# Local attention in smaller blocks: 32 queries by 64 keys in place of 64 by 96, one score tile a chunk, and a pipeline of four stations in place of five

## The chip, the cores and the metric

The kernel runs on one core of one Trainium2 chip. A core has a matrix engine (TensorE, PE in the profile, with PEld for its weight loads), three engines for elementwise work (VectorE or DVE, ScalarE or ACT, GpSimd or POOL), and SyncE (SP), which here only issues transfers. The metric is the device time of one launch in microseconds, and less is better. The three timed runs of the kernel before took 3015.64, 3015.70 and 3017.27 us; their median is 3015.7 us.

## The reference

Two blocks are computed for 4 sequences of 512 tokens with 128 features, all in float32. The first holds a gated scan, a mixture of experts and a causal attention; it is not touched by the change except in how two of its PSUM tiles are named. The second, where most of the time goes, is six layers of local attention with 16 heads of 64 features, each followed by a small feed-forward network. This is its attention:

```python
def local_attention(q, k, v):              # window w = 32
    bq, bk, bv = blocks of 32 tokens
    bk2, bv2 = (look(bk), look(bv))        # each block with the one ahead of it: 64 keys
    mask = (it < jb) | (it > jb + w) | (jb == -1)
    sim = einsum('bhwie,bhwje->bhwij', bq, bk2) * 8.0
    attn = softmax(where(mask, -max, sim), -1)
    return einsum('bhwij,bhwje->bhwie', attn, bv2)

def attn_layer(x, Wqkv, qs, ksc, Wo):
    q, k, v = split(x @ Wqkv, 3)           # 16 heads x 64 each
    q, k = l2norm(q) * qs, l2norm(k) * ksc
    q = q*cos*scale + rotate_half(q)*sin*scale
    k = k*cos/scale + rotate_half(k)*sin/scale
    return local_attention(q, k, v) as rows of 1024, @ Wo
```

A query i sees the keys from i - 32 to i. The layer's input is `x` with half its features shifted by one token, and its output is added to `x`. The feed-forward network is a layer norm, a gated GELU of width 341 and a product back to 128 features, added to the same state.

## The kernel before

The state of each sequence lies transposed in SBUF (`sA[b]`, 128 features by 513 columns). A layer is worked in chunks of 128 tokens, so there are 6 layers x 4 sequences x 4 chunks = 96 chunks (`Chunk`). A loop of 96 + 4 rounds (line 786) makes one new chunk a round and moves five chunks a station further; `xe` is the newest and `xa` the oldest. The order in which the loop calls the methods is the order of the instructions on every engine: lines 858 to 863 tie each instruction to the one before it on its engine. So nothing overtakes, and an instruction that waits holds up all that stands behind it on its engine.

What a chunk goes through:

- `rotate(j)`, j = 2, 3 for the keys and 0, 1 for the queries, 8 heads each. One 128x512 product on PE into PSUM (line 539, tile `q`, tag `mm`), two multiplications on DVE (`lt`, lines 547 and 551), their sum on POOL (`ro`, line 556), the squares on ACT (`sq`, line 558, after the DVE readers), and their sums by head on DVE (`ss`, line 559). `norms` raises the sums to the power -1/2 on POOL (line 569), and `scale_keys` multiplies the keys on POOL (line 576).
- `values(j)`: two more 128x512 products (line 586), copied by ACT into `vr` (line 590). `spread` issues three transfers on SP's queue (lines 595 to 597), which lay the keys' values of each block of 64 queries, 96 rows, at partition 0 (`vk`, two sets).
- `window` and `turn(j)`: four 128x128 transposes a call on PE (line 134, tile `tp_r`, tag `tr`) and one copy to `qT` or `kT`.
- `scores(g)`, for 8 heads at a time: a mask is put into two PSUM banks by two bf16 products with an identity (line 621, tag `S`), and 16 products of 64 features x 64 queries x 96 keys are added (line 630). `lm` is the row maximum of 8 heads (line 637) and `lnb` its scaled negative. `exponentials` calls ACT once a head, 128x96 (line 650).
- `flip(g, k)`: four transposes, one head each (line 662, tag `tr`), and a copy of 96x512 to `lpT` (line 516).
- `weigh(g)`: 16 products of 96 keys x 64 queries x 65 columns (line 674, tag `S`); the 65th column gives the sum. DVE divides (`lr` line 680, `on` line 682).
- `lift(j)`: four transposes and a copy by ACT to `oT`; `project`: 8 products with `Wo` (line 698) and two additions to `sA` (line 704).

`feedforward` is a generator of eight parts. It starts once the last chunk of a sequence has been projected, and `advance()` runs one part at fixed places, eight places in four rounds; so its work comes once in four rounds.

[...] Tags `mm` and `tr` have two tiles of one bank each, tag `S` two tiles of two banks. A tile is handed out again only when all readers of its former content are done. A product in float32 shows as two records on PE, and a transpose as one.

Of the kernel before, what the change touches and what calls it, by code (L numbers as in the profile page):

```python
# [35 lines left out]
QB = 64  # L36
# [25 lines left out]
M_BAND = 4 * KB  # L62
# [4 lines left out]
def fused(ctx: ExitStack, tc: tile.TileContext, a: dict, out: bass.AP):  # L67
# [7 lines left out]
    def psum(tag, name):  # L75
        return pp.tile([P, 2, 512] if tag == "S" else [P, 512], F32, tag=tag, name=name)
# [68 lines left out]
    with ExitStack() as stage:  # L145
# [153 lines left out]
        def expert_out(b, e, hT, pr, acc):  # L299
            y = psum("S", f"y{b}_{e}")  # L300
# [26 lines left out]
    with ExitStack() as stage:  # L327
# [39 lines left out]
        def softmax(b, h):  # L367
# [6 lines left out]
            for i2 in range(NC // 2):  # L374
                S = psum("S", f"gs{b}_{h}_{i2}")
# [73 lines left out]
    with ExitStack() as stage:  # L449
# [20 lines left out]
        vr = [sp.tile([P, HEADS, DH + 1], F32, name=f"vr{i}") for i in range(2)]  # L470
        vk = [[sp.tile([KB, HEADS, DH + 1], F32, name=f"vk{i}_{k}") for k in range(2)] for i in range(2)]
        for v in vr:
            nc.vector.memset(v[:, :, DH : DH + 1], 1.0)
        for v in vk:
            nc.vector.memset(v[0], 0.0)
# [42 lines left out]
        class Chunk:  # L518


            def __init__(self, n, l, b, c, w, last):
# [4 lines left out]
                self.VK = vk[n % 2]  # L526
                self.ss = sm.tile([P, 2 * HEADS], F32, tag="ss", name=f"ss{self.tag}")
                self.rot = {}
                self.S = {}
                self.nb = {}  # L530
                self.P = {}
                self.pT = {}
                self.on = {}

            def rotate(self, j):

                tag = f"{self.tag}_{j}"
                q = psum("mm", f"q{tag}")
# [3 lines left out]
                )  # L542
                cs = self.w["rot"][:, 2 * (j // 2), self.c, :]
# [13 lines left out]
                sq = wk.tile([P, 512], F32, tag="sq", name=f"sq{tag}")  # L557
                nc.scalar.activation(sq, q, AF.Square)  # L558
                nc.vector.tensor_reduce(  # L559
                    self.ss[:, j * 8 : j * 8 + 8], heads(sq), AX.X, ALU.add  # L560
# [23 lines left out]
            def values(self, j):  # L584
# [5 lines left out]
                nc.scalar.copy(self.V[:, j * 8 : j * 8 + 8, 0:DH], heads(v))  # L590

            def spread(self):

                if self.c:
                    nc.sync.dma_start(self.VK[0][0:WIN], self.last.V[P - WIN :])
                nc.sync.dma_start(self.VK[0][WIN:], self.V[0:QB])
                nc.sync.dma_start(self.VK[1], self.V[QB - WIN :])

            def window(self):

                self.qT = wk.tile([P, HEADS // 2, P], F32, tag="qT", name=f"qT{self.tag}")
# [14 lines left out]
            def scores(self, g):  # L616

                gt = f"{self.tag}_{g}"
                S = psum("S", f"ls{gt}")[:, :, 0 : 4 * KB]
# [4 lines left out]
                S = S.rearrange("p a (s k) -> p a s k", s=4)  # L624
                for s in range(4):
                    for blk in range(2):

                        for par in range(2):
                            lo, to = par * 64, blk * QB
                            nc.tensor.matmul(  # L630
                                S[to : to + QB, par, s, :],
                                lhsT=self.qT[lo : lo + 64, 4 * g + s, to : to + QB],
                                rhs=self.kT[lo : lo + 64, 4 * g + s, to : to + KB],
                                start=False, stop=s == 3,
                            )
                m = sm.tile([P, 4, 2], F32, tag="lm", name=f"lm{gt}")
# [3 lines left out]
                nb = sm.tile([P, 8], F32, tag="lnb", name=f"lnb{gt}")  # L640
                nc.vector.tensor_tensor(  # L641
                    nb, m.rearrange("p s a -> p (s a)"), self.rq[:, 8 * g : 8 * g + 8], ALU.mult
                )
                self.S[g], self.nb[g] = S, nb
                self.P[g] = wk.tile([P, 8, KB], F32, tag="lp", name=f"lp{gt}")

            def exponentials(self, g, of):
# [138 lines left out]
        for i in range(len(todo) + 4):  # L786
# [29 lines left out]
            if xb:  # L816
                xb.lift(0)
# [151 lines left out]
```

## Time and profile before

One execution was profiled. Its own time was 3016.47 us, and the span from its first to its last instruction 3014.7 us.

| | busy us | share of the span |
|---|---|---|
| PE (matmul) | 2558.3 | 85% |
| PEld (weight loads, beside PE) | 1679.1 | 56% |
| DVE | 1950.1 | 65% |
| ACT | 1476.6 | 49% |
| POOL | 1401.7 | 46% |
| one stretch of four rounds of the layers (1502.40 to 1594.60 us) | 92.2 | |

The mean granted TensorE clock was 0.933. The layers begin at 746.8 us with the first `q` product, and fill the rest of the span. There the work repeats every four rounds. Busy shares count a matmul from its start to its modelled end, so records that overlap each other count once; the rate at which products start is read from the times at which groups of them begin.

### The profile page before, as it was taken

The numbers are of one execution on the slowest core, as the hardware profiler recorded it, in microseconds if no ns is written. First come the engines' busy times: TensorE is split into PE (matmuls) and PEld (weight loads), VectorE is DVE, ScalarE is ACT, GpSimd is POOL, SyncE is SP. The second block draws the span as 40 slices with busy tenths as digits, with TensorE's granted clock in tenths as the row PEclk, the third lists the DMA queues.
The fourth block names the chain that finished last, engine by engine and source line by source line (L and its number), as shares of the span: only waits on it lengthen the run. The fifth ranks groups of instructions, "written<-read, shape, count | busy, mean of one in ns | idle before, by whom it ended". The sixth has DMA issues, their size and how long they took to land.

```text
span 3014.7 us, 56751 instructions
## 1 busy us (share of the span) xinstructions
PE 2558.3 (85%) x22640; PEld 1679.1 (56%) x22640; DVE 1950.1 (65%) x4218; ACT 1476.6 (49%) x3417; POOL 1401.7 (46%) x1002
## 2 busy tenths in 40 slices
PE   3899888887779888888888898888888888988886
PEld 1567545554456555555555565555555555655553
DVE  6344466666676666766667666666666676666764
ACT  1111133333556555555555565555555555655553
POOL 2000011111766555665556555565655565555550
PEclk7799989999899999999999999999999999999998
DMA  5000000000112111121112111121111211111110
GB/s 168 1 1 1 1 1 1 1 1 1 42 32 77 32 31 33 42 67 33 31 40 67 33 42 31 31 68 41 32 32 32 75 34 31 41 32 31 37 37 17
DMA packets 44963, 103.92 MB, mean 34 GB/s; under 512 B 5526, under 2 KB 23196, under 8 KB 43804
## 3 DMA queue, kind: packets, MB, share of 16 engines
q1 hardware_dynamic: 41852, 97.27, 12.3%
q8 instruction: 178, 2.92, 0.4%
q10 hardware_dynamic: 2848, 3.03, 0.3%
q14 instruction: 85, 0.70, 0.1%
HBM read 25.75 MB, written 1.05 MB: 9 GB/s over the span
## 4 chain that ended last, share of the span: by engine, by line
PE 33%; DVE 22%; ACT 17%; issue 2%; ACTq 0%; DMA 0%; DVEq 0%; POOL 0%; POOLq 0%
PE q L539 7%; PE ly L698 6%; ACT lp L650 6%; PE lv L586 5%; DVE lt L547 5%; ACT sq L558 5%; PE tp_r L134 4%; DVE lt L551 4%; DVE ss L559 3%; PE ls L630 3%; DVE lm L637 3%; DVE on L682 2%; PE lo L674 2%; PE lpt L662 2%; PE tp_on L134 1%
## 5 line engine op out<-in xcount | busy, mean ns | idle before, releaser
L556 POOL TENSOR_TENSOR ro<-lt,lt 128x512 f32<-128x512 f32 x384 | 487.5, 1270 | 721.8 <-DVE lt L551 369.3
L558 ACT ACTIVATE sq<-q 128x512 f32<-128x512 f32 x384 | 232.1, 604 | 644.8 <-DVE lt L551 603.1
L650 ACT ACTIVATE lp<-ls,lnb,rn 128x96 f32<-128x96 f32 x1536 | 529.0, 450 | 4.1 <-DVE lnb L641 3.8
L559 DVE TENSOR_REDUCE ss<-sq 128x8 f32<-128x512 f32 x384 | 263.3, 686 | 352.4 <-ACT sq L558 352.4
L539 PE MATMUL q<-wqkv,sA 128*128 128x512 f32 x768 | 430.5, 644 | 4.7 <-DVE fh L738 2.9
L134 PEld LDWEIGHTS tp_r<-ident,ro 128*128 128x128 f32 x1536 | 197.6, 151 | 265.4 <-issue 156.0
L547 DVE TENSOR_TENSOR lt<-q,rot 128x512 f32<-128x512 f32 x384 | 265.4, 691 | 106.4 <-PE q L539 105.0
L134 PE MATMUL tp_r<-ident,ro 128*128 128x128 f32 x1536 | 254.8, 293 | 81.9 <-DVE st_f L115 48.1
L662 PEld LDWEIGHTS lpt<-ident,lp 128*96 128x96 f32 x1536 | 180.6, 130 | 242.3 <-issue 139.6
L569 POOL TENSOR_TENSOR rn<-rn,neg_half 128x16 f32<-128x16 f32 x96 | 278.9, 2905 | 64.9 <-DVE rn L566 64.8
L569 POOL TENSOR_TENSOR rk<-rk,neg_half 128x16 f32<-128x16 f32 x96 | 278.8, 2905 | 27.6 <-DVE rk L566 27.6
L662 PE MATMUL lpt<-ident,lp 128*96 128x128 f32 x1536 | 233.4, 282 | 64.0 <-DVE lpT L516 60.8
L551 DVE TENSOR_TENSOR lt<-q,rot 128x512 f32<-128x512 f32 x384 | 261.0, 680 | 0.0
L516 DVE COPY lpT<-lpt 96x512 f32<-96x512 f32 x288 | 192.0, 681 | 105.6 <-PE lpt L662 105.5
L630 PE MATMUL ls<-kT,qT 64*64 64x96 f32 x6144 | 185.7, 262 | 53.7 <-ACT qT L516 53.7
L674 PE MATMUL lo<-vk,lpT 96*64 96x65 f32 x6144 | 223.8, 225 | 1.1 <-ACT lpT L516 1.1
L630 PEld LDWEIGHTS ls<-kT,qT 64*64 64x64 f32 x6144 | 149.8, 142 | 128.3 <-issue 65.5
L698 PE MATMUL ly<-oT,lwo 128*128 128x128 f32 x1536 | 194.4, 280 | 26.9 <-ACT vr L590 26.9
L674 PEld LDWEIGHTS lo<-vk,lpT 96*64 96x64 f32 x6144 | 197.0, 138 | 35.7 <-issue 34.3
L586 PE MATMUL lv<-wqkv,sA 128*128 128x512 f32 x384 | 207.4, 644 | 3.2 <-ACT sq L558 3.2
L590 ACT COPY vr<-lv 128x512 f32<-128x512 f32 x192 | 113.8, 593 | 179.4 <-PE lv L586 179.4
L698 PEld LDWEIGHTS ly<-oT,lwo 128*128 128x128 f32 x1536 | 178.9, 192 | 37.8 <-ACT vr L590 32.5
(178 smaller groups left out, 4195.8 us busy)
## 6 DMA issues: line engine op xcount, KB each, us to landing
vk<-vr SPq DMA_DIRECT2D x96, 390.0 KB, 4.0
vk<-vr SPq DMA_DIRECT2D x96, 260.0 KB, 3.4
vk<-vr SPq DMA_DIRECT2D x72, 130.0 KB, 2.3
wqkv<-in_lwqkv_dram SPq DMA_DIRECT2D x6, 1536.0 KB, 10.0
ew<-in_ew_dram SPq DMA_DIRECT2D x16, 256.0 KB, 6.3
lwo<-in_lwo_dram SPq DMA_DIRECT2D x6, 512.0 KB, 10.9
lw<-in_lw_dram SPq DMA_DIRECT2D x6, 341.0 KB, 10.2
cst<-in_cst_dram ACTq DMA_DIRECT2D x1, 1028.0 KB, 5.3
```

Of the source, the lines that this page charges most:

```text
L134: nc.tensor.transpose(tp[:, c * P : (c + 1) * P], i[:, c, :], ident)
L539: nc.tensor.matmul(q, lhsT=self.xs, rhs=self.w["qkv"][:, j * 512 : (j + 1) * 512], start=True, stop=True,)
L547: nc.vector.tensor_tensor(heads(t1), heads(q), cs[:, None, :].to_broadcast([P, 8, DH]), ALU.mult)
L551: nc.vector.tensor_tensor(swapped(t2), swapped(q)[:, :, ::-1, :], sn[:, None].to_broadcast([P, 8, 2, 32]), ALU.mult,)
L556: nc.gpsimd.tensor_tensor(self.rot[j], t1, t2, ALU.add)
L558: nc.scalar.activation(sq, q, AF.Square)
L569: nc.gpsimd.tensor_tensor(r, r, neg_half.to_broadcast([P, HEADS]), ALU.pow)
L630: nc.tensor.matmul(S[to : to + QB, par, s, :], lhsT=self.qT[lo : lo + 64, 4 * g + s, to : to + QB], rhs=self.kT[lo : lo + 64, 4 * g + s, t ...
L650: nc.scalar.activation(self.P[g][:, i, :], self.S[g][:, i % 2, i // 2, :], AF.Exp, bias=self.nb[g][:, i : i + 1], scale=self.rq[:, 8 * g + ...
L662: nc.tensor.transpose(pt[0:KB, i * P : (i + 1) * P], self.P[g][:, 4 * k + i, :], ident)
L674: nc.tensor.matmul(o[to : to + QB, i // 4, i % 4, :], lhsT=self.pT[g][:, i, to : to + QB], rhs=self.VK[blk][:, 8 * g + i, :], start=True, ...
L698: nc.tensor.matmul(y, lhsT=self.w["o"][:, j, :], rhs=self.oT[:, j, :], start=j == 0, stop=j == INNER // P - 1,)
```

## The change

The blocks become 32 queries by 64 keys (`QB` 32, `NB` 4 blocks a chunk). With 64 keys, two heads of one block fill 128 partitions.

- `mask` opens one tile `S` for all 16 heads with two bf16 products of 512 columns. `scores(g)` adds 32 products of 64 features x 32 queries x 64 keys for 8 heads, and `largest` takes one maximum over 1024 columns and one `lnb` for 16 heads. Each exponential is 128x64.
- `flip(g)` transposes two heads at once, four transposes for 8 heads and two calls a chunk in place of four; its copy is 128x512.
- `weigh(g)` is 32 products of 64 keys x 32 queries x 65 columns. `vk` is one set of four tiles with two heads' halves on 128 partitions, and `spread` issues ten transfers a chunk (eight for the first chunk of a sequence) in place of three.
- In PSUM `S` and `o` have one tile of two banks each. `qT`, `lp` and `lpT` in SBUF have one buffer each.
- `rotate` is split: `query` holds the product and the squares on ACT, which now stand ahead of the two DVE multiplications that read the same PSUM tile.
- The rounds have four stations (`xp` queries, `xt` turns, `xs` scores and values, `xw` weighing and projection), 96 + 3 in all, with a new order. One `lift` copy, and one `turn` copy and one `flip` copy in every fourth round, are on DVE.
- `feedforward` takes its statistics from the SBUF copy `n` in place of the PSUM tile, and its gates' tile from `o`.

```diff
-QB = 64
+QB = 32
+NB = P // QB
-M_BAND = 4 * KB
+M_BAND = 8 * KB
     def psum(tag, name):
-        return pp.tile([P, 2, 512] if tag == "S" else [P, 512], F32, tag=tag, name=name)
+        if tag in ("S", "o"):
+            return pp.tile([P, 2, 512], F32, tag=tag, name=name, bufs=1)
+        return pp.tile([P, 512], F32, tag=tag, name=name)
...
-            y = psum("S", f"y{b}_{e}")
+            y = psum("So"[e % 2], f"y{b}_{e}")
...
-                S = psum("S", f"gs{b}_{h}_{i2}")
+                S = psum("So"[i2], f"gs{b}_{h}_{i2}")
...
-            def rotate(self, j):
+            def query(self, j):
                 tag = f"{self.tag}_{j}"
-                q = psum("mm", f"q{tag}")
+                self.q[j] = q = psum("mm", f"q{tag}")
                 nc.tensor.matmul(
                     q, lhsT=self.xs, rhs=self.w["qkv"][:, j * 512 : (j + 1) * 512],
                     start=True, stop=True,
                 )
+                self.sq[j] = wk.tile([P, 512], F32, tag="sq", name=f"sq{tag}")
+                nc.scalar.activation(self.sq[j], q, AF.Square)
+
+            def rotate(self, j):
+                tag, q = f"{self.tag}_{j}", self.q[j]
...
                 nc.gpsimd.tensor_tensor(self.rot[j], t1, t2, ALU.add)
-                sq = wk.tile([P, 512], F32, tag="sq", name=f"sq{tag}")
-                nc.scalar.activation(sq, q, AF.Square)
                 nc.vector.tensor_reduce(
-                    self.ss[:, j * 8 : j * 8 + 8], heads(sq), AX.X, ALU.add
+                    self.ss[:, j * 8 : j * 8 + 8], heads(self.sq[j]), AX.X, ALU.add
                 )
...
             def spread(self):
-                if self.c:
-                    nc.sync.dma_start(self.VK[0][0:WIN], self.last.V[P - WIN :])
-                nc.sync.dma_start(self.VK[0][WIN:], self.V[0:QB])
-                nc.sync.dma_start(self.VK[1], self.V[QB - WIN :])
+                for par in range(2):
+                    lo = par * KB
+                    if self.c:
+                        nc.sync.dma_start(vk[0][lo : lo + WIN], self.last.V[P - WIN :, par])
+                    nc.sync.dma_start(vk[0][lo + WIN : lo + KB], self.V[0:QB, par])
+                    for r in range(1, NB):
+                        k0 = r * QB - WIN
+                        nc.sync.dma_start(vk[r][lo : lo + KB], self.V[k0 : k0 + KB, par])
...
+            def mask(self):
+                self.S = S = psum("S", f"ls{self.tag}")
                 for par in range(2):
                     nc.tensor.matmul(
                         S[:, par], lhsT=ident_h, rhs=bands[min(self.c, 1)], start=True, stop=False
                     )
+            def scores(self, g):
+                S = self.S.rearrange("p a (s k) -> p a s k", k=KB)
+                for s in range(4 * g, 4 * g + 4):
+                    for r in range(NB):
                         for par in range(2):
-                            lo, to = par * 64, blk * QB
+                            lo, to = par * 64, r * QB
                             nc.tensor.matmul(
                                 S[to : to + QB, par, s, :],
-                                lhsT=self.qT[lo : lo + 64, 4 * g + s, to : to + QB],
-                                rhs=self.kT[lo : lo + 64, 4 * g + s, to : to + KB],
+                                lhsT=self.qT[lo : lo + 64, s, to : to + QB],
+                                rhs=self.kT[lo : lo + 64, s, to : to + KB],
...
+            def flip(self, g, engine):
+                pt = psum("tr", f"lpt{self.tag}_{g}")
                 for i in range(4):
+                    s = 4 * g + i
                     nc.tensor.transpose(
-                        pt[0:KB, i * P : (i + 1) * P], self.P[g][:, 4 * k + i, :], ident
+                        pt[:, i * P : (i + 1) * P],
+                        self.P[:, 2 * s : 2 * s + 2, :].rearrange("p a k -> p (a k)"), ident,
                     )
...
             def weigh(self, g):
+                o = psum("o", f"lo{self.tag}_{g}")[:, :, 0 : 4 * (DH + 1)]
+                for i in range(4):
+                    for r in range(NB):
+                        for par in range(2):
+                            lo, to = par * KB, r * QB
+                            nc.tensor.matmul(
+                                o[to : to + QB, par, i, :],
+                                lhsT=self.pT[lo : lo + KB, 4 * g + i, to : to + QB],
+                                rhs=vk[r][lo : lo + KB, 4 * g + i, :], start=True, stop=True,
+                            )
...
-            stats = statistics(chunks(tp), f"f{tag}")
+            stats = statistics(n, f"f{tag}")
...
-            two = psum("S", f"fg{tag}")
+            two = psum("o", f"fg{tag}")
```

The new round, which replaces lines 786 to 854:

```python
for i in range(len(todo) + 3):
    ...
    xw, xs, xt, xp = (at(i - k) or idle for k in (3, 2, 1, 0))
    k = (i - 3 - 3) % NC
    xs.mask(); xw.weigh(0); xw.divide(0); xs.scores(0)
    xw.weigh(1); xw.divide(1); xs.scores(1); xs.largest(); xt.window()
    xs.values(0); xw.lift(0, nc.scalar); xs.exponentials(range(4)); xp.query(2)
    xw.lift(1, nc.vector); xp.rotate(2); xs.values(1); xs.spread(); xs.exponentials(range(4, 8))
    xt.turn(2, nc.scalar); xp.query(3); xs.exponentials(range(8, 12))
    xp.rotate(3); xp.scale_keys(); xt.turn(3, nc.scalar); xw.project()
    xp.query(0); xs.exponentials(range(12, 16)); xp.rotate(0); xt.turn(0, nc.scalar)
    if k in (0, 1, 2): advance()
    xt.turn(1, nc.vector if k == 1 else nc.scalar)
    if k in (1, 2): advance()
    xp.query(1); xs.flip(0, nc.vector); xp.rotate(1); xp.scale_queries()
    if k in (0, 2, 3): advance()
    xs.flip(1, nc.vector if k == 1 else nc.scalar)
```

## The prediction

> **What bounds the kernel now.** I read the page's busy table and chain first, then the groups, then the timeline of PE over one round, then DVE and ACT in the same window, then the waits.
>
> ```profile
> PE 2558.3 (85%) x22640; PEld 1679.1 (56%) x22640; DVE 1950.1 (65%) x4218; ACT 1476.6 (49%) x3417; POOL 1401.7 (46%) x1002
> ...
> PE 33%; DVE 22%; ACT 17%; issue 2%; ACTq 0%; DMA 0%; DVEq 0%; POOL 0%; POOLq 0%
> ```
>
> PE is the fullest engine, but the chain changes engine often: PE waits for others every round.
>
> ```profile
> 1506.48 1.02 PE L539 MATMUL q<-wqkv,sA 128*128 128x512 f32 x2
> 1507.34 0.60 PE L662 MATMUL lpt<-ident,lp 128*96 128x128 f32 x4
> 1507.78 1.95 PE L698 MATMUL ly<-oT,lwo 128*128 128x128 f32 x16
> 1509.57 0.60 PE L134 MATMUL tp_r<-ident,ro 128*128 128x128 f32 x4
> ...
> 1511.39 1.15 PE L674 MATMUL lo<-vk,lpT 96*64 96x65 f32 x32
> 1512.48 0.66 PE L134 MATMUL tp_on<-ident,on 128*128 128x128 f32 x4
> 1512.97 0.49 PE L621 MATMUL ls<-mask_h,ident_h 128*128 128x384 bf16 x2
> 1513.73 0.89 PE L630 MATMUL ls<-kT,qT 64*64 64x96 f32 x32 [0.27 <-ACT qT L516]
> 1514.56 1.12 PE L539 MATMUL q<-wqkv,sA 128*128 128x512 f32 x2
> ```
>
> From start to start, a 128x512 float32 product takes PE 0.86 us, four transposes 0.44, `ly` 1.79, a weighing group 1.09, the mask pair about 0.49, a score group 0.83. A round without feed-forward sums to 16 us: six products 5.2, 16 turns' transposes 1.75, 16 of `lpt` 1.75, 8 of `tp_on` 0.98, masks 0.98, scores 1.66, weighing 2.18, `ly` 1.79. The maxima at 830.34, 850.52 and 870.71 us give 20.2 us for such a round. With the feed-forward network four rounds take 92.2 us (1503.61 to 1595.77), 23.0 each. The difference of 4 us is waiting and the lowered clock:
>
> ```profile
> 1502.40:1594.60 92.20, 80.95 (x826) 53.66 (x826) 63.30 (x127) 53.86 (x125) 53.94 (x38) 0.94 0.14 35
> ...
> ACT sq L558 <- DVE lt L551: 603.1, 264, 5.4
> DVE ss L559 <- ACT sq L558: 352.4, 384, 2.4
> PE tp_r L134 <- DVE st_f L115: 48.1, 21, 2.7
> DVE lt L547 <- PE q L539: 105.0, 239, 2.1
> ```
>
> The columns of the first line are PE, PEld, DVE, ACT, POOL, clock, DMA share, GB/s. The waits show a serial chain in each `rotate`: product, two DVE passes, square on ACT, sum on DVE.
>
> [...] the 32 score records begin (0.89 - 0.24) / 31 = 21 ns apart although a 96-column stream needs 80 ns (0.83 ns a column, from 0.86 us for two records of 512), which is 80 over 4 tiles. Weighing, with 2 tiles, shows (1.15 - 0.22) / 31 = 30 ns against 54 / 2. [...] `tp_on` behind weighing takes 0.49 against 0.44. [...]
>
> **The change, part by part.** *Small products.* 64 columns are 53 ns, over 8 tiles 6.7 ns a record. A group of 64 records is 0.45 us. Four groups stand together: 1.8 us [...], against 3.84; saved 1.8. The 8-tile form is not in this trace. If only 4 tiles run at once a group is 0.9, and the four are 3.6, a saving of nothing; I take 0.45, as both present groups follow the number of tiles. *Flips*: two calls fewer, 0.88. *Mask*: two 512-column products for four of 384, about 0.6 against 0.98, 0.38. Together PE needs 3.1 us less a chunk, 295 us over 96. That is what the change brings if PE's stalls stay as they are.
>
> *DVE.* One maximum of 1024 columns: 947 ns at 768 and 686 at 512 give 1.02 ns a column, so 1.21 against 1.9. Flips: from three copies to one, plus one of `lift`, 0.6 less. DVE then needs 12.4 us in a plain round. *ACT*: an exponential falls from a place of 0.32 us ((2.68 - 0.45) / 7) by 32 columns of 0.83 ns (368 ns at 128 columns, 688 at 512, line 390) to about 0.30; I use 0.31; 0.3 us a chunk less. *POOL* keeps 13.3 us (four sums 1.27, two powers 2.9, two scalings 1.04, one copy 0.40).
>
> *SP.* Ten transfers a chunk for three. They are issued 0.57 us apart (480 to 545 ns each), and 130 KB land after 2.3 us. The first needs only the last chunk's values; nine wait for the second value copy, behind which nothing but later weights stands on SP. 8 x 0.57 + 2.3 to 4 = 6.9 to 8.6 us after that copy. `vk` has one set, so weighing of the next round waits for it, with mask ahead of it and scores behind.
>
> *Order and buffers.* I walked one plain round by the new order, with PE's result read 0.27 us after its stream (1506.48 + 0.86 to `lt` at 1507.61), 0.61 a DVE place of 512 columns and 0.69 to its result, 0.46 to 0.49 an ACT place and 0.6 to its result. Zero is DVE's end of the round before; weighing 0 is done by then.
>
> DVE divides until 0.92; `o` has one tile, so weighing 1 starts at 0.97; DVE divides again 1.70 to 2.62; maximum to 3.75, `lnb` 3.94. PE goes on with value product, `tp_on`, query 2, `tp_on` to 4.62. ACT: copies to 4.07, four exponentials to 5.30, and only then `sq` 2 to 5.90. The square now stands ahead of DVE's readers, so `lt` starts at 5.93 and ends at 7.22. Query 3 needs that PSUM tile: 7.27 to 8.13; its square, behind four exponentials and a copy, ends at 9.0; DVE to 10.32, sum and `rk` to 10.95. `ly` ends 10.36; query 0 10.37 to 11.23; additions to `sA`; square to 12.10; DVE 12.13 to 13.96. ACT: four exponentials to 13.22, the `qT` copy to 13.80. `flip` 0 needs that PSUM tile: PE 13.85 to 14.29, DVE 14.56 to 15.17, then `rotate` 1 to 17.0 and `rn`. **The plain round is 17.1 us at full clock**, and it is DVE's chain through ACT and PE that closes it, with 4.7 us of gaps on DVE. Values land at about 14 to 15 and are needed at 15.3; POOL's 13.3 fit.
>
> The feed-forward parts stand in the last third of the round: in the first of four rounds statistics (4 x 0.45) and normalise (4 x 0.31) on DVE make 20.0; in the second `xn`, three gate products, the GELUs with a table load of 1.28 and two more DVE copies make 21.8; in the third a table load back (1.2 late on ACT), three more products and three DVE passes make 20.7; in the fourth `fy` and two passes of 0.75 make 18.6. Sum 81.1. About 7.6 us of each walk is PE time; at the granted 0.94 that is 0.4 more a round: **82.7 for four rounds against 92.2**.
>
> 23 such groups save 9.5 each, 218 us; the first rounds without feed-forward save some 2.7 each, about 11. The first block stays: `S` and `o` alternate as two `S` tiles did. The tail after the last projection (2974.4 us to the end, 40 us) is the same generator. One station less is worth nothing sure, as filling rounds are short. 230 us off 3016.5, the profiled execution, is 2786; against the median of 3015.7 it is **2785**.
>
> **The rivals.**
> - *PE stays the bound and its waits go too.* For it: DVE would be at 14.2 of 18.5 us, so a better fit than my walk is possible, and `tp_r` no longer stands behind `st_f`, 48.1 us in all. PE needs 16 - 3.1 + 2.1 (feed-forward, a quarter of 8.6) = 15.0, at 0.94 16.0; with 2.3 of waits 18.3 a round: 4.7 x 95 = 447 less, 2570. Against it: one-buffer tiles and squares behind exponentials.
> - *Values come late.* With a landing of 5 to 6 us more than reckoned (ten transfers sharing engines with each other; before, the longest of the three landed after 4.0), weighing starts at 19 or so in plain rounds: two us more in the plain ones, one in the others, 1.5 x 95 = 140 back: 2925. For it: single `vk`, under one round of slack against over one before.
> - *Slower: small tiles do not run eight at a time.* If a record starts only each 28 ns, two tiles at a time, a group is 1.8 us. PE, from `flip` 0 at 13.85 through mask and three groups to the maximum, then gets it at 22.9 where the walk had 19.6: 3.3 more a round, 24.0 against 23.0, and 3015.7 + 95 = 3110. [...] Against it: 21 ns already seen.
> - *No change* would need the waits to eat exactly what PE gives up.
>
> **How the numbers follow.** Chances: the walk 0.58, with its own range 2690 to 2880 (1 us a round either way); PE-bound and freer 0.16 (2570 to 2690); late values or another one-buffer wait 0.16 (2870 to 3005); slower 0.08; within 0.2%, which is about what a measurement here can tell from no change, 0.02. Two in ten are left out: the lower case under 2620 (0.05), the late case over 2940 (0.05), no change and slower (0.10). Faster 0.90, same 0.02, slower 0.08.
>
> **What would show it.** Right: score and weighing records 7 to 9 ns apart on average, a group some 0.45 to 0.6 us; four rounds of 80 to 86 us; DVE over 68% busy in the layers and PE's share by its records no higher; `lt` waiting for `sq` where `sq` waited for `lt`; DVE waiting for `lpt` and `lo`. Wrong: the first `lo` record waiting for a transfer by more than a us a round (late values), groups of 0.9 us or more (tiles not concurrent), [...] or rounds of 18 us with PE full.

## The result, and the profile after

The changed kernel takes 2993.7 us, the median of four runs (2989.2 to 3001.6), against 3015.7 us before: a ratio of 0.9929, with a 95% interval of 0.9907 to 0.9951. It is faster by 22 us where 230 were forecast. The profiled execution took 2995.5 us, its span 2993.6 us at a mean granted clock of 0.927.

These are the busy row and the shares of the chain on the page of the kernel after.

```profile
PE 2364.7 (79%) x33872; PEld 1536.6 (51%) x33968; DVE 1971.8 (66%) x3977; ACT 1357.4 (45%) x3275; POOL 1398.2 (47%) x1002
...
DVE 25%; PE 21%; ACT 20%; issue 5%; POOL 2%; DMA 1%; SPq 0%; DVEq 0%; POOLq 0%; ACTq 0%
```

DVE is now ahead of PE on the chain, as forecast. PE gave up 194 us of busy time, less than the 295 reckoned. DVE's busy time should have fallen: one maximum of 1024 columns in place of two of 768 takes 65 us less over all chunks, the copies of `lpT`, `qT` and `oT` 27 less, and `lnb` 14 less, together 106 us. It rose by 22.

Four rounds from one maximum to the fourth after it, in the table of stretches (PE, PEld, DVE, ACT and POOL busy, clock, DMA share, GB/s):

```profile
1505.35:1594.28 88.93, 71.54 (x1295) 46.93 (x1299) 64.33 (x117) 48.60 (x117) 53.75 (x37) 0.96 0.19 49
```

This stretch is a good one: 22.2 us a round, where all 95 rounds from the first to the last maximum have a mean of 22.8. The forecast was 82.7 for four, 20.7 a round. So 2.1 us a round, 200 us in all, is what has to be found.

The waits that answer to those shown before:

```profile
PE lo L688 <- DVE on L699: 211.7, 96, 5.7
DVE oT L519 <- PE tp_on L137: 192.5, 96, 5.0
ACT sq L544 <- PE q L539: 145.0, 148, 2.1
DVE lr L697 <- PE lo L688: 131.8, 98, 5.4
DVE lt L552 <- ACT sq L544: 126.4, 160, 1.8
```

`lt` waits for `sq` where `sq` waited for `lt`. PE stands 2.2 us a round ahead of the second weighing group, which needs the first division. And two small groups have grown (busy us, mean ns, idle before):

```profile
L569 DVE TENSOR_SCALAR rn<-ss 128x16 f32<-128x16 f32 x96 | 86.7, 903 | 3.3
L569 DVE TENSOR_SCALAR rk<-ss 128x16 f32<-128x16 f32 x96 | 76.8, 800 | 3.3
```

They are the same 16-column instructions as before, where they took 174 ns in the median (line 566; min/median/max in ns, first and last start in us):

```profile
L566 DVE TENSOR_SCALAR rk<-ss x96: 174/174/177, 754.3 to 2920.7; 128x16 f32<-128x16 f32 x96
L566 DVE TENSOR_SCALAR rn<-ss x96: 174/174/1115, 759.7 to 2935.8; 128x16 f32<-128x16 f32 x96
```

That is about 130 us more of DVE: the 106 us saved above, and the rise of 22.

**One plain round against the walk.** Only the first few of the 95 rounds are plain, but it was a plain one that the prediction walked in full. DVE's timeline of the second round without feed-forward, from its maximum to the next (start, us, idle before):

```profile
803.33 1.23 DVE L652 TENSOR_REDUCE lm<-ls 128x16 f32<-128x1024 f32 x1
804.59 0.18 DVE L656 TENSOR_TENSOR lnb<-lm,rn 128x16 f32<-128x16 f32 x1
806.63 0.69 DVE L519 COPY oT<-tp_on 128x512 f32<-128x512 f32 x1 [1.86 <-PE tp_on L137]
807.75 0.69 DVE L552 TENSOR_TENSOR lt<-q,rot 128x512 f32<-128x512 f32 x1 [0.43 <-ACT sq L544]
...
813.66 0.69 DVE L552 TENSOR_TENSOR lt<-q,rot 128x512 f32<-128x512 f32 x1
...
815.96 0.69 DVE L519 COPY lpT<-lpt 128x512 f32<-128x512 f32 x1 [0.42 <-PE lpt L675]
...
818.48 1.00 DVE L569 TENSOR_SCALAR rn<-ss 128x16 f32<-128x16 f32 x1
819.39 0.19 DVE L697 RECIPROCAL lr<-lo 128x8 f32<-128x8 f32 x1
819.62 0.69 DVE L699 TENSOR_TENSOR on<-lo,lr 128x512 f32<-128x512 f32 x1
821.65 0.21 DVE L697 RECIPROCAL lr<-lo 128x8 f32<-128x8 f32 x1 [1.34 <-PE lo L688]
821.90 0.69 DVE L699 TENSOR_TENSOR on<-lo,lr 128x512 f32<-128x512 f32 x1
822.52 1.23 DVE L652 TENSOR_REDUCE lm<-ls 128x16 f32<-128x1024 f32 x1
```

Counted from the maximum (the walk had it at 2.54 from its own zero, and 17.1 for the round):

| | walk | measured | late by |
|---|---|---|---|
| `oT` copy | 2.35 | 3.30 | 0.95 |
| `lt` of query 0 | 9.59 | 10.33 | 0.74 |
| `flip` 0 copy | 12.02 | 12.63 | 0.61 |
| first division (`lr`) | 14.55 | 16.06 | 1.51 |
| second division | 16.25 | 18.32 | 2.07 |
| next maximum | 17.10 | 19.19 | 2.09 |

The whole middle of the round, four `rotate` calls and a flip, ran as walked, or 0.3 us shorter. The time is lost in three places: between the maximum and `oT` (0.95), at `rn` (0.82 more than the 0.09 that the walk gave it), and between the two divisions (2.26 for 1.70).

**At `rn`.** The timeline of DVE and POOL there:

```profile
818.18 2.48 POOL L561 TENSOR_TENSOR ro<-lt,lt 128x512 f32<-128x512 f32 x2
818.48 1.00 DVE L569 TENSOR_SCALAR rn<-ss 128x16 f32<-128x16 f32 x1
```

The row merges two sums of 1.24 us on POOL; the first ends at 819.4, and `rn` ends at 819.48. Of the 96 `rn`, 95 began while POOL was busy with a sum or a scaling and ended within 40 ns of the end of that instruction; of the 96 `rk`, 94. The two multiplications ahead of them also overlap POOL's work and keep their 0.68 us. So a 16-column instruction that begins beside one of POOL's sums or scalings lasts until that ends; the two that began beside its power (one `rn`, one `rk`) kept 0.17 us. In the kernel before POOL was idle at that moment (94 of 96 `rn`, all 96 `rk`).

**Behind the weighing wait.** The stretch around the waiting group and the value product behind it, and one of the same round without such a wait:

```profile
800.50:805.50 5.00, 4.33 (x135) 3.21 (x136) 2.75 (x5) 0.61 (x2) 3.49 (x3) 0.66 0.07 17
815.00:819.00 4.00, 2.95 (x137) 2.34 (x138) 3.54 (x6) 1.78 (x4) 3.92 (x4) 1.00 0.05 13
```

The mean clock is 0.66 in one, which is half speed for part of it, and full in the other. At full clock a weighing group takes 0.60 us from its first record to the first of the scores behind it, and the two records of a value product 1.02 (at 806.43 in this round):

```profile
816.77 0.82 PE L688 MATMUL lo<-vk,lpT 64*32 64x65 f32 x60
817.37 0.23 PE L641 MATMUL ls<-kT,qT 64*32 64x64 f32 x1
```

Behind the wait they take longer (the first score starts at 802.01, 0.84 us behind the weighing group's start):

```profile
801.17 1.13 PE L688 MATMUL lo<-vk,lpT 64*32 64x65 f32 x61 [2.35 <-DVE on L699]
...
802.05 1.25 PE L641 MATMUL ls<-kT,qT 64*32 64x64 f32 x63
...
803.22 1.64 PE L589 MATMUL lv<-wqkv,sA 128*128 128x512 f32 x2
```

Between the first maximum and the last, the trace has 56 spells at half clock, 270 us in all.

### The profile page after: what moved, and what is told of

It is laid out like the page before. It is cut to its first block, busy times and chain, and to the rows that moved or that the text cites. A ratio compares the mean times of both kernels' runs of the same rounds, so it can differ in the third digit from the quotient of the medians.

```text
span 2993.6 us, 80281 instructions
## 1 busy us (share of the span) xinstructions
PE 2364.7 (79%) x33872; PEld 1536.6 (51%) x33968; DVE 1971.8 (66%) x3977; ACT 1357.4 (45%) x3275; POOL 1398.2 (47%) x1002
## 4 chain that ended last, share of the span: by engine, by line
DVE 25%; PE 21%; ACT 20%; issue 5%; POOL 2%; DMA 1%; SPq 0%; DVEq 0%; POOLq 0%; ACTq 0%
ACT lp L665 9%; DVE lt L552 5%; PE lv L589 5%; PE q L539 5%; DVE lt L556 5%; ACT sq L544 4%; PE lo L688 3%; DVE ss L562 3%; DVE rn L569 3%; PE ls L641 2%; DVE on L699 2%; ACT vr L593 2%; PE fg L743 2%; DVE lpT L519 2%; ACT kT L519 1%
## 5 line engine op out<-in xcount | busy, mean ns | idle before, releaser
L665 ACT ACTIVATE lp<-ls,lnb,rn 128x64 f32<-128x64 f32 x1536 | 506.7, 440 | 2.5 <-DVE lnb L656 2.2
L688 PE MATMUL lo<-vk,lpT 64*32 64x65 f32 x12288 | 182.5, 238 | 237.0 <-DVE on L699 211.7
L688 PEld LDWEIGHTS lo<-vk,lpT 64*32 64x32 f32 x12288 | 148.2, 112 | 297.4 <-issue 260.8
L137 PE MATMUL tp_r<-ident,ro 128*128 128x128 f32 x1536 | 227.4, 274 | 68.5 <-ACT qT L519 65.5
L589 PE MATMUL lv<-wqkv,sA 128*128 128x512 f32 x384 | 252.9, 746 | 2.6 <-issue 1.8
L641 PE MATMUL ls<-kT,qT 64*32 64x64 f32 x12288 | 201.8, 248 | 27.7 <-issue 27.5
L539 PEld LDWEIGHTS q<-wqkv,sA 128*128 128x128 f32 x768 | 123.2, 199 | 166.3 <-ACT vr L593 78.3
L579 POOL TENSOR_TENSOR ro<-ro,rk 128x512 f32<-128x512 f32 x192 | 196.1, 1042 | 7.5
L519 DVE COPY oT<-tp_on 128x512 f32<-128x512 f32 x96 | 66.4, 692 | 192.5 <-PE tp_on L137 192.5
L137 PEld LDWEIGHTS tp_on<-ident,on 128*128 128x128 f32 x768 | 113.5, 162 | 135.7 <-issue 126.2
```

The costliest lines, as they stand in the source:

```text
L137: nc.tensor.transpose(tp[:, c * P : (c + 1) * P], i[:, c, :], ident)
L539: nc.tensor.matmul(q, lhsT=self.xs, rhs=self.w["qkv"][:, j * 512 : (j + 1) * 512], start=True, stop=True,)
L589: nc.tensor.matmul(v, lhsT=self.xs, rhs=self.w["qkv"][:, (4 + j) * 512 : (5 + j) * 512], start=True, stop=True,)
L665: nc.scalar.activation(self.P[:, i, :], self.S[:, i % 2, i // 2 * KB : (i // 2 + 1) * KB], AF.Exp, bias=self.nb[:, i : i + 1], scale=self. ...
L688: nc.tensor.matmul(o[to : to + QB, par, i, :], lhsT=self.pT[lo : lo + KB, 4 * g + i, to : to + QB], rhs=vk[r][lo : lo + KB, 4 * g + i, :], ...
```

## The experiments

Times are medians of four runs (twelve in run 11), and differences are to the changed kernel's 2993.7 us where nothing else is said. The kernel before took 3014.8 to 3018.6 us beside them. Ratios are to the kernel before.

**1 and 2: what the wait behind POOL costs.** In the first run POOL does the small instruction; in the second DVE keeps it, and POOL's order is turned.

```diff
-                nc.vector.tensor_scalar(
+                nc.gpsimd.tensor_scalar(
                     r, self.ss[:, j * HEADS : (j + 1) * HEADS], 1e-24, square, ALU.max, ALU.mult
```

> After the change, with the two 16-column norms instructions of a chunk (max and scale, groups rn and rk) on POOL ahead of its power instead of on DVE. Theory (a DVE tensor_scalar of 16 columns that starts while POOL runs its sum waits until that sum ends, and rn stands directly ahead of the next round's divisions): the 0.83 us of rn leave DVE's chain, rk's is hidden behind the wait for the query product, so about 0.7 us a round over 95 rounds, 2994 - 65 = 2925 to 2940; if rk's share counts too, 2870. Rival (DVE is not what closes the round; PE's late and slow weighing does): within 10 us of 2994. Same computation.

```diff
-                nc.gpsimd.tensor_tensor(self.rot[j], t1, t2, ALU.add)
                 nc.vector.tensor_reduce(
                     self.ss[:, j * 8 : j * 8 + 8], heads(self.sq[j]), AX.X, ALU.add
                 )
+                if j == 3:
+                    self.rk = self.norms(1, "rk", 1.0)
+                if j == 1:
+                    self.rq = self.norms(0, "rn", QK_SCALE**-2)
+                nc.gpsimd.tensor_tensor(self.rot[j], t1, t2, ALU.add)
...
-                r = self.norms(1, "rk", 1.0)
+                r = self.rk
...
-            xp.scale_queries()
```

> After the change, the same instructions, but POOL's order turned: the sum ro of the pair that norms closes stands behind the power, so POOL is idle when DVE runs rn and rk. Theory (DVE waits for POOL's running instruction): rn and rk fall from 0.83 and 0.81 us to about 0.17, and the time falls as in the run with the norms on POOL, by 50 to 70 us, 2925 to 2945. Rival (the instruction itself is that long here, or DVE waits for its write): rn and rk keep 0.8 us and the time stays near 2994. Same computation.

They took 2960.7 us (ratio 0.9811, 0.9785 to 0.9837) and 2964.3 us (0.9821, 0.9796 to 0.9846): 33 and 30 us less, half of what was expected. The second settles the mechanism, as nothing but POOL's order differs and `rk` falls with it. The two groups there:

```profile
L573 DVE TENSOR_SCALAR rn<-ss 128x16 f32<-128x16 f32 x96 | 48.6, 506 | 3.3
L573 DVE TENSOR_SCALAR rk<-ss 128x16 f32<-128x16 f32 x96 | 16.8, 175 | 3.3
```

`rk` is back at 0.17 us, but `rn` is not always: POOL now runs later, and 28 of the 96 `rn` meet the sum of the pair before (DVE and POOL in a plain round of this run):

```profile
848.51 1.30 DVE L573 TENSOR_SCALAR rn<-ss 128x16 f32<-128x16 f32 x1
848.52 1.26 POOL L568 TENSOR_TENSOR ro<-lt,lt 128x512 f32<-128x512 f32 x1
```

That leaves 0.40 us a round for `rn`, 38 us in all, of which 30 arrived. In the first run a wait of 0.89 us ahead of the next `lt` takes the place of `rk`: `rk` was hidden, as expected. There DVE's waits for weighing grew from 132 to 148 us, which takes part of what `rn` gave; the rest of the shortfall is open.

**3: the second weighing group's wait for the first division.** The last row sum and `rn` go behind that division (`xz` is the chunk that was begun in the round before).

```diff
                 nc.gpsimd.tensor_tensor(self.rot[j], t1, t2, ALU.add)
+                if j != 1:
+                    self.sums(j)
+
+            def sums(self, j):
                 nc.vector.tensor_reduce(
                     self.ss[:, j * 8 : j * 8 + 8], heads(self.sq[j]), AX.X, ALU.add
                 )
...
+            xz = xt
...
             xs.mask()
             xw.weigh(0)
             xw.divide(0)
+            xz.sums(1)
+            xz.scale_queries()
             xs.scores(0)
...
             xp.rotate(1)
-            xp.scale_queries()
```

> After the change, with the last row sum ss and rn of a round moved behind the first division of the next round, where DVE waits for the second weighing group. Theory (the second weighing group waits 2.2 us a round for the first division, which stands behind rotate; DVE then idles about 1.45 us between its two divisions): PE's wait for the division falls from 212 us to under 80, ss and rn fill DVE's idle time, rn ends POOL's overlap as well: 1.3 to 1.5 us a round, 2994 - 133 = 2850 to 2880. Rival (the clock at half speed after the wait is what costs, and the wait only moves): 0 to 50 us less, 2945 to 2994. Same computation.

2954.1 us (0.9782, 0.9746 to 0.9817): 40 us less, so the rival's range held. PE's wait for the division fell from 212 to 119 us and `rn` to a mean of 214 ns, yet most of the 133 us did not come. The half clock stayed, as the rival has it: 45 spells, 239 us. A new wait is in PE's timeline, inside a group of scores, where the trace shows no semaphore that it waits for:

```profile
803.04 0.34 PE L645 MATMUL ls<-kT,qT 64*32 64x64 f32 x8
804.23 0.78 PE L645 MATMUL ls<-kT,qT 64*32 64x64 f32 x54 [0.85 <-issue]
```

What is left, as I read it, is the supply of PE's own instructions. The trace also holds the transfers of a queue that the page calls `instruction`; its rows, before and after (transfers, MB, share of 16 engines' time):

```profile
q8 instruction: 178, 2.92, 0.4%
```

```profile
q8 instruction: 269, 4.41, 0.6%
```

These are transfers of 16,384 bytes each. PE shows 68,728 records after (products, weight loads, semaphores and drains), which is about 256 for each of them. A transfer takes 1.07 us in the median. Of the gaps inside small groups in run 3, some 110 us in all against 44 in the changed kernel, the middle eight tenths end 1.3 to 1.6 us after such a transfer has ended. A chunk's four groups are 128 products, that is 512 PE instructions in some 2.4 us (four times the 0.60 us of a group at full clock); the 64-wide blocks took 256 in 3.8 us.

**4: the clock.** Products that are thrown away fill PE's wait. The mask pair moves behind the first weighing group, and four more mask products go ahead of it.

```diff
-                for par in range(2):
+                for i in range(6):
                     nc.tensor.matmul(
-                        S[:, par], lhsT=ident_h, rhs=bands[min(self.c, 1)], start=True, stop=False
+                        S[:, i % 2], lhsT=ident_h, rhs=bands[min(self.c, 1)],
+                        start=True, stop=i < 4,
                     )
...
-            xs.mask()
             xw.weigh(0)
             xw.divide(0)
+            xs.mask()
```

> After the change, with the mask put in between the first weighing group and the scores and four more bf16 mask products of 512 columns (about 0.24 us each at full clock, they are overwritten by the last pair) in PE's idle time before the second weighing group. Theory (the idle time makes the granted clock fall, and weighing, scores and the first value product then run at half speed): the clock in the layers rises from 0.93 to over 0.97, the first value product takes 0.86 us instead of 1.5 and more, and the time falls by 0.3 to 0.8 us a round, 2915 to 2965. Rival (the clock falls for another reason, or the round is closed elsewhere): the same time or up to 30 us more, 2990 to 3025. Computes the same, with products that are thrown away.

2945.3 us (0.9766, 0.9744 to 0.9788): 48 us less by giving PE more to do (480 records of mask products for 96, 0.25 us of busy time each). The clock rose to 0.962 (over 0.97 was expected), the spells at half clock fell to 16, 82 us, and a record of the value products fell from 746 to 639 ns:

```profile
L589 PE MATMUL lv<-wqkv,sA 128*128 128x512 f32 x384 | 213.6, 639 | 1.9 <-issue 1.9
```

The gain is in the rounds with feed-forward, where DVE had been longest between weighing 0 and its division: in the second round of four `oT` now comes 2.5 us behind the maximum, in the third too, where it took 4.2 and 4.0 (medians). Plain rounds became slower, from 19.2 to 20.2 us; why is open. The move of the mask pair was not tried without the filler.

**5: the same filler in small products.** 64 score products in place of four mask products, ahead of the mask pair.

```diff
...
+                for s in [0, 1, 2, 3] * 2:
+                    for r in range(NB):
+                        for par in range(2):
+                            lo, to = par * 64, r * QB
+                            nc.tensor.matmul(
+                                S[to : to + QB, par, s, :],
+                                lhsT=self.qT[lo : lo + 64, s, to : to + QB],
+                                rhs=self.kT[lo : lo + 64, s, to : to + KB],
+                                start=True, stop=True,
+                            )
```

> As the run with four mask products as filler, but the filler before the mask pair is 64 small score products (256 PE instructions with their weight loads, about 1.1 us at full clock by 0.56 us a group) in place of 4 mask products (8 instructions, about 1 us). Theory (PE is fed its instructions in transfers of 16 KB, 256 instructions, and bursts of small products outrun them: in the runs before, each stall inside a group ended 1.2 to 1.6 us after such a transfer did): a burst grows from two such transfers to three, stalls inside the groups grow by 1 us a round or more, and the time rises from 2945 to 3030 to 3130. Rival (PE's time alone counts, and the stalls have another cause): within 20 us of 2945. Computes the same, with products that are thrown away.

3229.4 us (1.0700, 1.0679 to 1.0721): 284 us more than run 4, 3.0 us a round, beyond the range expected of the supply of instructions, and far outside the rival's. PE in one burst of this run:

```profile
1510.43 0.45 PE L655 MATMUL ls<-kT,qT 64*32 64x64 f32 x30
1512.37 0.51 PE L655 MATMUL ls<-kT,qT 64*32 64x64 f32 x34 [1.49 <-issue]
...
1513.34 0.59 PE L655 MATMUL ls<-kT,qT 64*32 64x64 f32 x28
1515.94 0.84 PE L655 MATMUL ls<-kT,qT 64*32 64x64 f32 x34 [2.02 <-issue]
```

Two groups of the same 64 records stop in the middle for 1.5 and 2.0 us. To size this in each kernel, I took every gap of more than 0.35 us between the starts of two PE records in the layers, by the time since the last transfer on that queue ended, and summed them:

| us of gaps that end so long after a transfer | 0.9 to 1.2 us | 1.2 to 1.5 us | 1.5 to 1.8 us |
|---|---|---|---|
| before | 23 | 21 | 27 |
| after | 54 | 93 | 57 |
| run 3 | 27 | 137 | 50 |
| run 4 | 39 | 89 | 40 |
| run 5 | 29 | 329 | 77 |

Before there is no peak. In the changed kernel it stands some 40 us above its neighbours, in run 3 about 100, in run 5 about 275. So by this count the gaps that are read as waiting for instructions are worth about 40 us in the changed kernel (a sum of gaps, not all of it on the chain), and more in runs 3 and 5. With 256 instructions of small products in 3.8 us, as before, there is no peak; with 512 in 2.4 us there is one. That PE waits there for what these transfers bring is my reading: the traces show when the transfers and the gaps end, and no wait between them.

**6: one part undone, the square behind the multiplications.**

```diff
             def query(self, j):
...
-                self.sq[j] = wk.tile([P, 512], F32, tag="sq", name=f"sq{tag}")
-                nc.scalar.activation(self.sq[j], q, AF.Square)
             def rotate(self, j):
...
                 nc.gpsimd.tensor_tensor(self.rot[j], t1, t2, ALU.add)
+                self.sq[j] = wk.tile([P, 512], F32, tag="sq", name=f"sq{tag}")
+                nc.scalar.activation(self.sq[j], q, AF.Square)
```

> After the change, with one of its parts undone: the square of each query product stands behind the two DVE multiplications again, on ACT and by the PSUM tile's readers. Theory of the prediction (squares ahead make DVE wait: lt waits 126 us for sq): lt starts 0.4 to 0.9 us earlier in three places of a round, but the row sum then waits for the square, 0.5 to 0.9 us in each; the balance is a loss of 0 to 0.6 us a round, 2994 to 3050. Rival (undoing it frees DVE's chain): 2920 to 2970. Same computation.

3175.1 us (1.0520, 1.0498 to 1.0542): 181 us more, past both ranges. Its waits:

```profile
ACT sq L561 <- DVE lt L554: 530.8, 268, 7.0
DVE ss L562 <- ACT sq L561: 334.4, 384, 1.4
PEld q L539 <- ACT sq L561: 225.1, 192, 3.5
```

The first two are the waits of the kernel before. The third is the one that the expectation missed: the next query product needs the PSUM tile that the square reads last. Without this part the change would be 160 us slower than the kernel before.

**7 and 8: useful work in the wait.** The first value product stands between the first scores and the second weighing group; run 8 adds run 3's order and a third buffer for `vr`.

```diff
             xs.scores(0)
+            xs.values(0)
             xw.weigh(1)
...
-            xs.values(0)
             xw.lift(0, nc.scalar)
```

> After the change, with the first value product moved up into PE's wait between the first scores and the second weighing group (useful work in place of the filler, nothing thrown away). Theory (half clock after the wait, and 0.86 us of PE that stands between the maximum and tp_on): PE stays busy as with the filler, and the oT copy of DVE comes 0.5 to 1.5 us earlier behind the maximum: 0.6 to 1.2 us a round, 2994 - 57 to 115 = 2880 to 2937. Rival (its copy into vr now waits for transfers, or the stalls for instructions take it all): 2940 to 3000. Same computation.

> After the change, with two moves together: the last row sum and rn behind the next round's first division, and the first value product ahead of the second weighing group, and a third buffer for vr. Theory (with small products in bursts of two groups with a 512-column product between, instructions come in time; DVE's idle time between its divisions is filled; rn no longer meets POOL's sum): the gains of the two add up, 2954 - 57 to 115 = 2840 to 2900, and stalls inside small groups fall from 110 us to under 60. Rival (moves compete for the same gap): 2920 to 2955. Same computation.

2919.3 us (0.9673, 0.9648 to 0.9698) and 2882.0 us (0.9549, 0.9532 to 0.9566): 74 and 112 less, both in the theory's range. The gains of runs 3 and 7 add up, 40 + 74. What missed is the side remark on stalls: those inside small groups were still some 90 us, where under 60 were expected. Four rounds of run 8:

```profile
1472.86:1557.34 84.48, 69.90 (x1295) 45.37 (x1300) 62.63 (x117) 49.22 (x117) 51.86 (x37) 0.99 0.20 51
```

**9: two more moves.** On top of run 8 the output's first transposes stand between weighing and scores, and query product 2 with its square ahead of the second transposes and the exponentials.

```diff
             xw.weigh(1)
+            xw.lift(0, nc.scalar)
             xw.divide(1)
...
-            xw.lift(0, nc.scalar)
-            xs.exponentials(range(4))
             xp.query(2)
+            xs.exponentials(range(4))
             xw.lift(1, nc.vector)
```

> As the run with both moves (2882), with two more: the first four transposes of the output stand between the second weighing group and the second scores, and query product 2 with its square stands ahead of the other transposes and of the first four exponentials. Theory (DVE's chain still closes the round; behind the maximum it idles 0.9 us until tp_on and 0.4 to 0.9 us until the square, and small products in bursts of one group meet fewer instruction stalls): 0.7 to 1.2 us a round, 2882 - 67 to 115 = 2767 to 2815. Rival (PE's order now puts the product ahead of tp_on and instruction stalls take the rest): 2850 to 2890. Same computation.

2862.6 us (0.9482, 0.9468 to 0.9496), 19 less than run 8, where 67 to 115 were expected: the rival. Two rows of one plain round say why, one of DVE and one of PE:

```profile
826.82 0.69 DVE L552 TENSOR_TENSOR lt<-q,rot 128x512 f32<-128x512 f32 x1 [1.67 <-ACT sq L544]
```

```profile
819.89 0.70 PE L539 MATMUL q<-wqkv,sA 128*128 128x512 f32 x1
821.50 0.70 PE L539 MATMUL q<-wqkv,sA 128*128 128x512 f32 x1 [0.91 <-issue]
```

In plain rounds the first multiplication mostly came 1.3 us earlier behind the maximum than in run 8, and DVE gave 0.9 of that back at the next `rotate`, whose product waits for a PSUM tile (its wait grew from 0.76 to 1.66 us). And a query product stops for 0.91 us between its two records, with no semaphore to wait for. This is the fastest version that was run, 5.2% under the kernel before and 4.4% under the changed one.

**10: do the terms of runs 2 and 4 add up?** Both edits together.

> After the change, POOL's order turned and the four mask products as filler, both together. If DVE's wait behind POOL (29 us alone) and the half clock (48 us alone) are separate terms of one chain: 2994 - 77 = 2905 to 2930. If they share the same stretch, or the stalls for instructions grow where PE waits less: 2935 to 2965. Computes the same, with products that are thrown away.

2935.2 us (0.9719, 0.9701 to 0.9736): 59 us less, not 78, so they share a part. `rn` has a mean of 507 ns here, as in run 2.

**11: the square first, in the kernel before.** The one part whose undoing cost 181 us, done alone.

```diff
+                sq = wk.tile([P, 512], F32, tag="sq", name=f"sq{tag}")
+                nc.scalar.activation(sq, q, AF.Square)
                 cs = self.w["rot"][:, 2 * (j // 2), self.c, :]
...
                 nc.gpsimd.tensor_tensor(self.rot[j], t1, t2, ALU.add)
-                sq = wk.tile([P, 512], F32, tag="sq", name=f"sq{tag}")
-                nc.scalar.activation(sq, q, AF.Square)
```

> The kernel before, with one part of the change alone: in rotate the square on ACT stands ahead of the two DVE multiplications that read the same PSUM tile. Theory (undoing this part of the change cost 181 us, as each row sum then waits for a square that waits for two multiplications; the kernel before has the same chain, with 352 us of ss waiting for sq): 100 to 180 us less, 2835 to 2915, so that the rest of the change brings a loss. Rival (PE, 85% busy, bounds the kernel before): 2960 to 3020. Same computation.

3018.9 us against 3018.6, a ratio of 0.9996 (0.9986 to 1.0006): nothing. Its waits turned round (`lt` for `sq` 479 us, `sq` for `lt` gone), and the time did not notice. The kernel before is not closed by this chain, and the changed one is.

## Why the prediction was wrong

Right were the direction, the bound that takes PE's place and most of the walk. Small products do run side by side: 64 records from 816.77 to 817.37 are 9.4 ns each, where the walk had 6.7 (and 53 for 64 columns alone, from 0.86 us for two records of 512), and the group took 0.60 us for 0.45; the rival of two tiles at a time (1.8 us a group) is out. Values are not late: PE waited 2.3 us in all for the transfers of `vk`, so that rival is out too. PE is not the bound, as run 4 gave it more work and the time fell. DVE's chain through ACT and PE closes the round, and its middle was right to 0.3 us.

Four terms of the sum were wrong or missing:

- *"then `rotate` 1 to 17.0 and `rn`"*, with the first division at 17.09: the walk took the short time of the kernel before. It is 0.90 us in the mean and 0.83 in the median, because the POOL instruction that it lasts as long as, mostly a sum of 1.27 us, has begun 0.48 us ahead of it in the median (0.3 in the plain round shown). In the old order POOL was idle then; that the new order changes which POOL instruction runs beside a DVE instruction was not considered. Taken off the path this was worth 30 to 33 us, half of the 0.7 us a round expected; in run 2 other meetings of the two engines took the rest.
- *"at the granted 0.94 that is 0.4 more a round"*: a mean clock was spread over PE's time on the path. The clock does not fall evenly. It falls to half behind PE's longest wait (2.35 us just ahead of the plain round shown, where the clock was 0.50 from 800.9 to 804.3 us), and what stands there, weighing 1, scores 1, a value product and `tp_on`, is a stretch for which DVE waits. Between the first maximum and the last, 41 of 42 waits of 2.5 us or more were followed by half clock, and 11 of the 89 waits of 1.5 to 2.5 us; 37 of the 56 spells lasted 3.4 us. In the plain round shown it cost some 0.8 of the 0.95 us before `oT` (2.54 us in plain rounds where the clock stayed full) and part of the 0.56 between the divisions; filling the wait was worth 48 us.
- *"four groups stand together: 1.8 us"*: the walk counted time, not instructions. A burst of 512 PE instructions has gaps that I put down to the transfers that bring them. In the changed kernel they are about 40 us by the count above; in run 3 the gaps inside small groups were some 66 us more than that kernel's, where 93 us of the forecast did not come.
- *1.70 us from one division to the next*, measured 2.03 to 2.36 in plain rounds. With the filler, at nearly full clock, the median is still 2.06, with a wait of 1.1 us for weighing 1 where the walk had 0.8: the group was sized at 0.45 us and takes 0.60.

Two small sums of the prediction are off without weight: at 0.31 us sixteen exponentials save 0.16 us, not 0.3, and 7.6 us at a clock of 0.94 are 0.5 more, not 0.4. The 1.8 us saved of 3.84 on small products also allow 0.2 us beside the four groups, an estimate that no run was made for.

The four terms are places, not shares that add up: 30 and 48 us alone are 59 together. Of the 200 us that the rounds fell short, 112 came back with one order that shortens all three places (run 8) and 131 with the next (run 9), which also holds moves that the walk did not have. The rest is not settled run by run. The loss is in the rounds with feed-forward too: by their medians the four took 22.0, 24.7, 23.4 and 20.6 us, where the walk with its 0.4 had 20.4, 22.2, 21.1 and 19.0. Each lost about 1.6 us, and the second and third 0.7 to 0.9 more; with the filler these two fell by 1.5 and 1.1 us and the others by 0.3 or not at all. No run changed that network's order.

Why is the gain as large as 22 us? Run 11 against run 6: putting the square first is worth nothing in the kernel before and 181 us in the new one. So the rest of the change, smaller blocks, fewer buffers and a shorter pipeline together, moved the bound to DVE's chain, where only this reordering kept the change from a loss. Which of these parts did it was not tried.

## What to carry to other kernels

When a change makes one engine's share small, walk the chain that takes over with the durations of the new neighbourhood: a 0.17 us instruction can take 1.0 us because another engine's instruction now runs beside it, and a record of a value product 1.22 us in place of 0.60 because it runs at half clock behind a wait. Count small products as instructions too: bursts of them stopped here for 0.85 us (run 3) to 2.0 us (run 5) where the trace shows no semaphore to wait for; spread them between long products, and put useful work into PE's waits. A part that gives nothing alone may be the one that carries the whole, so test parts in both kernels.

## What the runs showed of the hardware

- Two PE fillers of about the same busy time by the recorded estimates (1.0 and 1.1 us a round), 8 instructions and 256, differ by 284 us over 96 rounds. Gaps inside a group end about 1.4 us after the end of a 16 KB transfer of instructions (median 1.37 to 1.43 us in the changed kernel and runs 3, 5 and 8).
- Work that is thrown away can make a kernel faster: 4 products a round, 48 us less.
- A DVE `tensor_scalar` of 16 columns lasts until POOL's running sum of 512 columns ends (1.0 us at `rn`), and is at its 0.17 us while POOL raises to a power (two cases in the trace of the changed kernel, and 21 `rn` in run 2). The `fn` instructions, 128 columns with operands by partition, kept 0.33 us beside the power, but in run 3 the first of four took 1.28 us in 21 of 24 cases: there POOL had just begun a sum of 512 columns.
